# Summing exp through halves added on GpSimd, and reordering the attention stretches

## Chip, cores and metric

The kernel runs on one core of a Trainium2 chip. The metric is the device time of that core in microseconds; lower is better. A run's time is a little longer than the span from the first to the last instruction in its trace.

## What is computed

Two graph layers follow each other on 64 graphs of 256 nodes with 256 features, all in float32. The first layer (adjacency attention, twice, then a feed-forward net with ReLU, with a layernorm after each half) is not touched. The change is in the attention of the second layer, which has eight heads of width 32 and an adjacency matrix that picks, for each pair of nodes, which of several value projections is used:

```python
q = (src @ Wq + bq) ... ; k = (src @ Wk + bk) ...          # split into 8 heads
scores = einsum('bhid,bhjd->bhij', q, k) / sqrt(dh)
attn = softmax(scores, axis=-1)
for r in range(R):
    v_r = (src @ Wv[r] + bv[r]) ...
    mask = (adj_matrix == r)
    out = out + einsum('bhij,bhjd->bhid', attn * mask, v_r)
x = layernorm(src + out @ Wo + bo)
x = layernorm(x + gelu(x @ W1 + b1) @ W2 + b2)
```

The adjacency here holds only 0 and 1, so the kernel uses two value projections: that of relation 0 for every pair of nodes, and the difference of the two on the pairs where the adjacency is 1.

## The kernel before

The 64 graphs are taken in 32 pairs. Each pair goes through one Python generator, `whole_way`: first `gat_layers` (the adjacency attention), then `feed_forward` with ReLU (called ff0 here), then `attention`, then `feed_forward` with Gelu (ff1). Loops over pairs are unrolled; what is generated is one long instruction stream for each engine, and each engine works through its stream in order.

The order of the streams is set by a planner, `in_turn`. It keeps three ways going. A way runs until it yields a triple: the TensorE time that the stretch just emitted is thought to take, a time that has to pass before the way may go on, and optionally a name. Only one way at a time may hold each of the names `gat`, `ff` and `attention`. The planner keeps a clock of its own made of these numbers; at each turn it takes a way that is ready by that clock, and a way in a feed-forward only if no other is ready. So while one pair is in attention, another is in a feed-forward and fills the time that attention's yields leave open: the stretches of `feed_forward` are eight of four matmul passes (`L308`, 1.72) and four of sixteen passes (`L319`, 3.44).

Attention works on four groups, n = 0 to 3, each of one graph b of the pair and one half c of the heads (four heads). The second layer's softmax is computed transposed: a score tile has keys j on the partitions and queries i along the free dimension, in two blocks jc of 128 keys. For one group:

- `scores` (`L360`): eight matmuls with a contraction of 32, four heads side by side, into four PSUM banks; then ScalarE takes exp of each bank into a tile `a` of 128 x 512 (`L365`), the two 256-wide halves being the two blocks of keys.
- `of_relation_1` (`L374`): VectorE multiplies each `a` by the adjacency, giving `m`.
- `sums` (`L381`): eight matmuls with `ones` (128 x 32) on the left sum exp over the keys, two blocks jc accumulated in PSUM, the sum being repeated on the head's 32 partitions.
- `products` (`L388`), with r = 0 on `a` and r = 1 on `m`: sixteen matmuls that add values into the other half of the same bank `po`.
- `divided` (`L394`, `L396`, `L398`): VectorE takes the reciprocal of the sums, keeps a figure that a later range test reads, and multiplies the products by the reciprocal into `oT`.

Around the groups stand the projections of queries and keys (`projected`, `L342`, evicted by ScalarE), the values of each block of keys (`values`, `L335`, evicted by VectorE at `L337` into the tile `v`), and `into_rows` (`L405`), which multiplies `oT` by the output weights, adds the rows (`L266`) and takes a layernorm. The layernorm's reciprocal root is done on GpSimd (`L276`), and so is the addition of a bias to rows when they are transposed (`L292`).

Before the change a stretch of the group loop emits the scores of the next group first, and then the sums and products of this one; the multiplications by the adjacency for the next group are emitted ahead of this group's `divided`:

```python
if not last:
    ahead = scores(*groups[n + 1])
po = bank()
sums(e, po)
products(c, 0, v, e, po)
products(c, 1, v, ms, po)
```

Of the kernel before, what the change touches and what calls it, by code (L numbers as in the profile page):

```python
# [10 lines left out]
F32 = mybir.dt.float32  # L11
# [4 lines left out]
ALU = mybir.AluOpType  # L16
AX = mybir.AxisListType

P = 128
# [10 lines left out]
def two_layers(ctx: ExitStack, tc: tile.TileContext, t: dict, out: bass.AP, flag: bass.AP):  # L30
# [9 lines left out]
    nc = tc.nc  # L40
    B, N, D = out.shape
    NPAIR = B // 2
    KC = D // P
# [4 lines left out]
    DH = D // H  # L48
    HQ = P // DH
# [25 lines left out]
    ones = const.tile([P, DH], F32, name="ones")  # L75
# [28 lines left out]
    with tc.tile_pool(name="setup", bufs=1) as setup, \  # L104
# [11 lines left out]
        for m in range(KC):  # L116
            pw = psetup.tile([P, 512], F32, name="pw")
            for c in range(KC):
                nc.tensor.matmul(pw[:, :D + 4], lhsT=w1T[:, c, m * P:(m + 1) * P], rhs=right[:, c],
                                 start=c == 0, stop=c == KC - 1)  # L120
# [17 lines left out]
    work = ctx.enter_context(tc.tile_pool(name="work", bufs=1))  # L138
# [3 lines left out]
    def bank():  # L142
        return psum.tile([P, 512], F32, name="ps")
# [30 lines left out]
    def done_with(name):  # L174
        del alone[name]

    def of_graph(b):
        return slice(2 * b, 2 * b + 2)
# [84 lines left out]
    def add_rows(y, p, b):  # L263

        rows = y[:, of_graph(b), :].rearrange("p k d -> p (k d)")
        nc.vector.tensor_tensor(rows, p, rows, ALU.add)  # L266

    def layernorm(r, gb, b):
        g, beta = gb
        st, mv = small.tile([P, 2, 6], F32, name="st"), small.tile([P, 2, 2], F32, name="mv")  # L270
        rstd = small.tile([P, 2], F32, name="rstd")
        for j in range(2):
            nc.vector.bn_stats(st[:, j, :], r[:, 2 * b + j, :])  # L273
            nc.vector.bn_aggr(mv[:, j, :], st[:, j, :])
        nc.vector.tensor_scalar(rstd, mv[:, :, 1], EPS, None, ALU.add)  # L275
        nc.gpsimd.tensor_tensor(rstd, rstd, mhalf[:, :2], ALU.pow)  # L276
        for j in range(2):
            row = r[:, 2 * b + j, :]
            nc.vector.scalar_tensor_tensor(row, row, mv[:, j, 0:1], g, op0=ALU.subtract, op1=ALU.mult)
        for j in range(2):  # L280
            row = r[:, 2 * b + j, :]
            nc.vector.scalar_tensor_tensor(row, row, rstd[:, j:j + 1], beta, op0=ALU.mult, op1=ALU.add)
# [11 lines left out]
    def rows_transposed(y, bias):  # L294
        yT = work.tile([P, KC, 512], F32, name="yT", bufs=2)
        for b in range(2):
            transposed(y, yT, bias, b)
            yield 0.5, 0.5 + b * 0.5, None
        return yT
# [31 lines left out]
    def values(v, jc, at, yT):  # L331

        ps = bank()
        for c in range(KC):
            nc.tensor.matmul(ps, lhsT=yT[:, c, at:at + P], rhs=wv[:, c].rearrange("p r m -> p (r m)"),  # L335
                             start=c == 0, stop=c == KC - 1)
        nc.vector.tensor_tensor(v[:, jc], ps, bv, ALU.add)  # L337

    def projected(to, c, yT, w, bias, scale):
        ps = bank()  # L340
        for d in range(KC):
            nc.tensor.matmul(ps, lhsT=w[:, d, c * P:(c + 1) * P], rhs=yT[:, d, :], start=d == 0, stop=d == KC - 1)  # L342
        nc.scalar.activation(to[:, c, :], ps, AF.Identity, bias=bias[:, c:c + 1], scale=scale)

    def attention(y, pair, adjT):


        yT = yield from rows_transposed(y, bo)
        qT, kT, oT = (work.tile([P, KC, 512], F32, name=n) for n in ("qT", "kT", "oT"))

        def values_tile():
            return work.tile([P, 2, 2 * D], F32, name="v", bufs=2)

        def scores(b, c):
            ps = [bank() for _ in range(HQ)]
            for jc in range(2):
                at = b * N + jc * P
                for o in range(HQ):
                    rows = slice(o * DH, (o + 1) * DH)
                    nc.tensor.matmul(ps[o][:, jc * N:(jc + 1) * N], lhsT=kT[rows, c, at:at + P],  # L360
                                     rhs=qT[rows, c, b * N:(b + 1) * N], start=True, stop=True)
            e = []
            for o in range(HQ):
                a = work.tile([P, 512], F32, name="a", bufs=2 * HQ)
                nc.scalar.activation(a, ps[o], AF.Exp)  # L365
                e.append(a)
            return e

        def of_relation_1(b, e):
            adj = adjT[:, of_graph(b), :].rearrange("p k n -> p (k n)")  # L370
            ms = []
            for a in e:
                m = work.tile([P, 512], F32, name="m", bufs=HQ + 2)
                nc.vector.tensor_tensor(m, a, adj, ALU.mult)  # L374
                ms.append(m)
            return ms

        def sums(e, po):
            for jc in range(2):
                for o in range(HQ):  # L380
                    nc.tensor.matmul(po[o * DH:(o + 1) * DH, N:], lhsT=ones, rhs=e[o][:, jc * N:(jc + 1) * N],  # L381
                                     start=jc == 0, stop=jc == 1)

        def products(c, r, v, ms, po):
            for jc in range(2):
                for o in range(HQ):
                    at = r * D + (c * HQ + o) * DH
                    nc.tensor.matmul(po[o * DH:(o + 1) * DH, :N], lhsT=v[:, jc, at:at + DH],  # L388
                                     rhs=ms[o][:, jc * N:(jc + 1) * N],
                                     start=r == 0 and jc == 0, stop=r == 1 and jc == 1)  # L390

        def divided(b, c, po):
            s = work.tile([P, N], F32, name="s", bufs=2)
            nc.vector.reciprocal(s, po[:, N:])  # L394
            junk = work.tile([P, N], F32, name="junk")
            nc.vector.scalar_tensor_tensor(junk, po[:, N:], 1.0, s, op0=ALU.mult, op1=ALU.add,  # L396
                                           accum_out=reach[:, pair, b * KC + c:b * KC + c + 1])
            nc.vector.tensor_tensor(oT[:, c, b * N:(b + 1) * N], po[:, :N], s, ALU.mult)  # L398

        def into_rows(b):  # L400
            ps = bank()
            for j in range(2):
                k = 2 * b + j
                for c in range(KC):
                    nc.tensor.matmul(ps[:, j * D:(j + 1) * D], lhsT=oT[:, c, k * P:(k + 1) * P], rhs=wo[:, c, :],  # L405
                                     start=c == 0, stop=c == KC - 1)
            add_rows(y, ps, b)
            layernorm(y, ln[2], b)

        groups = [(b, c) for b in range(2) for c in range(KC)]  # L410
        v = values_tile()
        projected(qT, 0, yT, wq, bqs, SCALE)
        projected(kT, 0, yT, wk, bk, 1.0)
        yield 3.44, 0.0, None
        values(v, 0, 0, yT)
        yield 1.72, 0.0, None
        e = scores(*groups[0])
        ms = of_relation_1(0, e)
        projected(qT, 1, yT, wq, bqs, SCALE)
        yield 3.0, 0.0, None  # L420
        projected(kT, 1, yT, wk, bk, 1.0)
        values(v, 1, P, yT)
        yield 3.44, 0.0, None
        for n, (b, c) in enumerate(groups):
            last = n == len(groups) - 1
            if not last:
                ahead = scores(*groups[n + 1])
            po = bank()
            sums(e, po)
            products(c, 0, v, e, po)  # L430
            products(c, 1, v, ms, po)
            if not last:
                e, ms = ahead, of_relation_1(groups[n + 1][0], ahead)
            divided(b, c, po)
            yield 3.1 if last else 4.1, 3.2 if last else 0.8, None
            if (b, c) == (0, KC - 1):
                v = values_tile()
                for jc in range(2):
                    values(v, jc, N + jc * P, yT)
                    yield 1.72, 0.0, None  # L440
            if n == 2:
                into_rows(0)
                yield 1.75, 0.0, None
        into_rows(1)
        done_with("attention")
        yield 1.75, 4.5, "ff"

    def whole_way(pair):
        yield 0.0, 0.0, "gat"
        xT, adjT, x = loaded.pop(pair)  # L450
        yield from gat_layers(pair, xT, adjT, x)
        yield from feed_forward(x, ff0, AF.Relu, ln[1])
        yield 3.44, 4.5, "attention"
        yield from attention(x, pair, adjT)
        yield from feed_forward(x, ff1, AF.Gelu, ln[3])
        nc.sync.dma_start(out[2 * pair:2 * pair + 2].rearrange("b (c p) d -> p (b c) d", p=P), x)
        yield 3.44, 0.0, None
# [439 lines left out]
```

## Time and profile before

| | us |
|---|---|
| median of 3 runs (lowest to highest) | 3452.53 (3450.27 to 3455.06) |
| the profiled execution | 3450.98 |
| its span, first to last instruction | 3449.2 |
| TensorE matmul busy in it | 3344.4 (97%) |
| VectorE busy | 1904.6 (55%) |
| ScalarE busy | 1371.0 (40%) |
| GpSimd busy | 481.5 (14%) |

The granted TensorE clock is 0.999 over the span. In lines of the profile, a group of instructions shows the line of the kernel, the engine, the operation, the tile written and the tiles read, the shapes and the count, then the busy time in us and the mean of one instruction in ns, then the idle time of the engine just before them and what ended it. A timeline line begins with the start in us and the length of the merged run of instructions. TensorE's float32 matmuls appear as two passes each, so that eight matmuls are sixteen records. "<-" in brackets names what was waited for.

### The profile page before, as it was taken

How to read it: one execution, taken by the hardware profiler on the slowest of the kernel's cores; microseconds unless marked ns; L12 is line 12 of the kernel's file. 1: busy time of each engine (PE TensorE's matmuls, PEld its weight loads, DVE VectorE, ACT ScalarE, POOL GpSimd, SP SyncE). 2: the span in 40 equal slices, each digit the busy share in tenths (PEclk: the TensorE clock that was granted, in tenths of full speed). 3: DMA queues.
4: the chain of work that ended last, by engine and by line, in shares of the span. 5: the costliest groups of instructions: out<-in, count | busy, mean ns of one | idle time of the engine just before them, and what ended most of it. 6: DMA issues, size and time to landing. Idle time of an engine off the chain costs nothing.

```text
span 3449.2 us, 47284 instructions
## 1 busy us (share of the span) xinstructions
PE 3344.4 (97%) x18698; PEld 2150.5 (62%) x18698; DVE 1904.6 (55%) x4825; ACT 1371.0 (40%) x2586; POOL 481.5 (14%) x646
## 2 busy tenths in 40 slices
PE   7999999999999999999999999999999999999998
PEld 5566665666656566565665666656666566565655
DVE  5655645556456564555645555465554655546455
ACT  4343343433434334343444434444253442534332
POOL 0201111011110111111111111111111111111110
PEclk9999999999999999999999999999999999999999
DMA  5000010000100001000000100001000010000000
GB/s 166 7 25 19 13 37 7 25 19 13 37 7 25 25 7 37 7 28 23 20 25 7 41 10 25 19 7 43 7 25 19 7 43 7 25 19 1 13 1 14
DMA packets 66868, 78.22 MB, mean 23 GB/s; under 512 B 3280, under 2 KB 57680, under 8 KB 66640
## 3 DMA queue, kind: packets, MB, share of 16 engines
q1 hardware_dynamic: 66640, 75.13, 7.0%
q8 instruction: 150, 2.46, 0.3%
q14 instruction: 78, 0.64, 0.1%
HBM read 58.34 MB, written 16.78 MB: 22 GB/s over the span
## 4 chain that ended last, share of the span: by engine, by line
PE 87%; ACT 9%; DVE 2%; DMA 1%; issue 0%; SPq 0%; POOL 0%; POOLq 0%; DVEq 0%
PE ps L319 26%; PE ps L308 23%; PE ps L342 7%; PE ps L335 6%; PE ps L388 6%; PE ps L360 4%; PE ps L381 4%; PE ps L253 3%; PE ps L405 3%; ACT L189 2%; ACT yT L290 2%; PE ps L241 2%; PE ps L227 2%; PE ps L289 1%; ACT ff L311 1%; DVE e L206 1%
## 5 line engine op out<-in xcount | busy, mean ns | idle before, releaser
L276 POOL TENSOR_TENSOR rstd<-rstd,mhalf 128x2 f32<-128x2 f32 x256 | 206.1, 805 | 2729.3 <-DVE rstd L275 2713.4
L308 PE MATMUL ps<-yT,w_L_gnn_W 128*128 128x512 f32 x1024 | 482.7, 602 | 14.2 <-ACT yT L290 12.5
L308 PE MATMUL ps<-yT,w_L_gnn_w_ff 128*128 128x512 f32 x1024 | 482.5, 602 | 14.1 <-ACT yT L290 12.5
L319 PE MATMUL ps<-w_L_gnn_w_ff,ff 128*128 128x256 f32 x2048 | 450.2, 379 | 0.0
L319 PE MATMUL ps<-w_L_gnn_W,ff 128*128 128x256 f32 x2048 | 449.9, 379 | 0.0
L319 PEld LDWEIGHTS ps<-w_L_gnn_W,ff 128*128 128x128 f32 x2048 | 389.1, 190 | 66.6 <-issue 15.3
L319 PEld LDWEIGHTS ps<-w_L_gnn_w_ff,ff 128*128 128x128 f32 x2048 | 389.0, 190 | 66.0 <-issue 14.8
L374 DVE TENSOR_TENSOR m<-a,adjT 128x512 f32<-128x512 f32 x512 | 327.0, 688 | 175.6 <-ACT a L365 134.9
L266 DVE TENSOR_TENSOR x<-ps,x 128x512 f32<-128x512 f32 x256 | 176.1, 688 | 444.3 <-PE ps L319 330.7
L311 ACT ACTIVATE ff<-ps,c_L_gnn_b_ff 128x512 f32<-128x512 f32 x256 | 176.0, 687 | 448.2 <-PE ps L308 448.2
L365 ACT ACTIVATE a<-ps 128x512 f32<-128x512 f32 x512 | 264.4, 602 | 216.3 <-PE ps L360 216.1
L337 DVE TENSOR_TENSOR v<-ps,b_L_gnn_bv 128x512 f32<-128x512 f32 x128 | 88.1, 689 | 400.5 <-PE ps L335 400.5
L308 PEld LDWEIGHTS ps<-yT,w_L_gnn_W 128*128 128x128 f32 x1024 | 183.0, 190 | 199.2 <-issue 174.1
L308 PEld LDWEIGHTS ps<-yT,w_L_gnn_w_ff 128*128 128x128 f32 x1024 | 183.1, 190 | 198.9 <-issue 174.2
L290 ACT ACTIVATE yT<-ps 128x512 f32<-128x512 f32 x192 | 110.2, 592 | 479.8 <-PE ps L289 479.8
L311 ACT ACTIVATE ff<-ps,c_L_gnn_b 128x512 f32<-128x512 f32 x256 | 175.9, 687 | 292.8 <-PE ps L308 292.4
L335 PE MATMUL ps<-wv,yT 128*128 128x512 f32 x512 | 235.4, 592 | 0.0
L229 ACT ACTIVATE xw<-ps 128x260 f32<-128x260 f32 x128 | 45.7, 379 | 456.0 <-PE ps L227 456.0
L394 DVE RECIPROCAL s<-ps 128x256 f32<-128x256 f32 x128 | 224.0, 1750 | 0.0
L273 DVE BATCH_NORM_STATS2 st<-x 128x6 f32<-128x256 f32 x512 | 192.7, 418 | 8.6
L206 DVE SCALAR_TENSOR_TENSOR e<-ps,ratio,up 128x256 f32<-128x256 f32 x256 | 115.7, 475 | 141.2 <-ACT up L201 141.2
L335 PEld LDWEIGHTS ps<-wv,yT 128*128 128x128 f32 x512 | 97.3, 190 | 122.5 <-issue 122.2
(81 smaller groups left out, 4290.1 us busy)
## 6 DMA issues: line engine op xcount, KB each, us to landing
xT<-in_xT SPq DMA_DIRECT2D x32, 512.0 KB, 4.6
adjT<-in_adjT SPq DMA_DIRECT2D x32, 512.0 KB, 3.9
x<-in_x SPq DMA_DIRECT2D x32, 512.0 KB, 4.2
out<-x SPq DMA_DIRECT2D x32, 512.0 KB, 3.2
w_L_gnn_w_ff<-in_L_gnn_w_ff SPq DMA_DIRECT2D x2, 1024.0 KB, 11.3
w_L_gnn_W<-in_L_gnn_W SPq DMA_DIRECT2D x2, 1024.0 KB, 7.0
wv<-in_L_gnn_Wv SPq DMA_DIRECT2D x2, 256.0 KB, 7.1
w_L_gnn_W1T<-in_L_gnn_W1T SPq DMA_DIRECT2D x1, 256.0 KB, 6.1
```

What stands on the lines that cost most here:

```text
L273: nc.vector.bn_stats(st[:, j, :], r[:, 2 * b + j, :])
L276: nc.gpsimd.tensor_tensor(rstd, rstd, mhalf[:, :2], ALU.pow)
L290: nc.scalar.activation(yT[:, :, b * N:(b + 1) * N], pt.rearrange("p (c n) -> p c n", c=KC), AF.Copy)
L308: nc.tensor.matmul(p1, lhsT=w1[:, c, m * P:(m + 1) * P], rhs=yT[:, c, :], start=c == 0, stop=c == KC - 1)
L311: nc.scalar.activation(h, p1, func, bias=b1[:, m:m + 1])
L319: nc.tensor.matmul(p2[:, j * D:(j + 1) * D], lhsT=f[m][:, k * P:(k + 1) * P], rhs=w2[:, m, :], start=m == 0, stop=m == NF - 1)
L335: nc.tensor.matmul(ps, lhsT=yT[:, c, at:at + P], rhs=wv[:, c].rearrange("p r m -> p (r m)"), start=c == 0, stop=c == KC - 1)
L342: nc.tensor.matmul(ps, lhsT=w[:, d, c * P:(c + 1) * P], rhs=yT[:, d, :], start=d == 0, stop=d == KC - 1)
L365: nc.scalar.activation(a, ps[o], AF.Exp)
L374: nc.vector.tensor_tensor(m, a, adj, ALU.mult)
L388: nc.tensor.matmul(po[o * DH:(o + 1) * DH, :N], lhsT=v[:, jc, at:at + DH], rhs=ms[o][:, jc * N:(jc + 1) * N], start=r == 0 and jc == 0, st ...
L394: nc.vector.reciprocal(s, po[:, N:])
```

## The change

The two 256-wide halves of each exp tile are first added on GpSimd into a new tile `halves` (128 x 256, six buffers), four additions for each group. The sum over keys is then one matmul with `ones` for each head instead of two accumulated ones. In the group loop a stretch now emits the group's own sums, products and `divided` first, and then the scores of the next group, their exp, the additions on GpSimd and the multiplications on VectorE. The yields, which the planner reads, are set anew.

```diff
+        def halves_added(e):
+            hs = []
+            for a in e:
+                h = work.tile([P, N], F32, name="halves", bufs=HQ + 2)
+                nc.gpsimd.tensor_tensor(h, a[:, :N], a[:, N:], ALU.add)
+                hs.append(h)
+            return hs
...
-        def sums(e, po):
-            for jc in range(2):
-                for o in range(HQ):
-                    nc.tensor.matmul(po[o * DH:(o + 1) * DH, N:], lhsT=ones, rhs=e[o][:, jc * N:(jc + 1) * N],
-                                     start=jc == 0, stop=jc == 1)
+        def sums(hs, po):
+            for o in range(HQ):
+                nc.tensor.matmul(po[o * DH:(o + 1) * DH, N:], lhsT=ones, rhs=hs[o], start=True, stop=True)
...
         e = scores(*groups[0])
-        ms = of_relation_1(0, e)
+        hs, ms = halves_added(e), of_relation_1(0, e)
...
         for n, (b, c) in enumerate(groups):
+            po = bank()
+            sums(hs, po)
+            products(c, 0, v, e, po)
+            products(c, 1, v, ms, po)
+            divided(b, c, po)
             last = n == len(groups) - 1
             if not last:
-                ahead = scores(*groups[n + 1])
-            po = bank()
-            sums(e, po)
-            products(c, 0, v, e, po)
-            products(c, 1, v, ms, po)
-            if not last:
-                e, ms = ahead, of_relation_1(groups[n + 1][0], ahead)
-            divided(b, c, po)
-            yield 3.1 if last else 4.1, 3.2 if last else 0.8, None
-            if (b, c) == (0, KC - 1):
+                e = scores(*groups[n + 1])
+                hs, ms = halves_added(e), of_relation_1(groups[n + 1][0], e)
+            if last:
+                yield 2.8, 4.8, None
+            elif n == 1:
+                yield 3.7, 0.0, None
                 v = values_tile()
                 for jc in range(2):
                     values(v, jc, N + jc * P, yT)
-                    yield 1.72, 0.0, None
-            if n == 2:
+                    yield 1.72, jc * 0.2, None
+            elif n == 2:
+                yield 3.7, 0.0, None
                 into_rows(0)
-                yield 1.75, 0.0, None
+                yield 1.75, 1.9, None
+            else:
+                yield 3.7, 3.6, None
```

## The prediction

> **What bounds the kernel now.** I read the page's busy times and its chain first, then the waits of TensorE, then the timeline of one attention. From the page:
>
> ```profile
> PE 3344.4 (97%) x18698; PEld 2150.5 (62%) x18698; DVE 1904.6 (55%) x4825; ACT 1371.0 (40%) x2586; POOL 481.5 (14%) x646
> ...
> PE 87%; ACT 9%; DVE 2%; DMA 1%; issue 0%; SPq 0%; POOL 0%; POOLq 0%; DVEq 0%
> ```
>
> TensorE carries 87% of the chain. Its waits sum to only some 92 us, nearly all in the other layer:
>
> ```profile
> PE ps L199 <- ACT rise L189: 29.6, 46, 0.9
> PE ps L308 <- ACT yT L290: 25.0, 34, 0.7
> PE ps L253 <- ACT xw L212: 21.0, 16, 3.0
> ```
>
> No line of attention's group loop (L360, L381, L388) is there. TensorE runs through attention without a gap, as this timeline of one group shows (scores, sums, two products):
>
> ```profile
> 1047.41 1.15 PE L360 MATMUL ps<-qT,kT 32*128 32x256 f32 x16
> 1048.48 1.07 PE L381 MATMUL ps<-a,ones 128*32 128x256 f32 x16
> 1049.37 1.05 PE L388 MATMUL ps<-a,v 128*32 128x256 f32 x16
> 1050.23 1.05 PE L388 MATMUL ps<-m,v 128*32 128x256 f32 x16
> ```
>
> From start to start the scores take 1.07 us, the sums 0.89, the products 0.86. So a matmul removed is time gained, if nothing new is waited for.
>
> **What the Trainium skill says.** "TensorE: Matmul & The Clock Gate", Part 3 (Packing small matmuls): matmuls on different column strips run side by side. The trace agrees: sixteen passes of 379 ns in 0.89 us, four at a time. "GPSIMD Engine Reference", Engine selection: a two-input elementwise operation is about twice as slow there as on VectorE. Here 0.73 against 0.48 us for 128x256, the one fused on VectorE. "SBUF — State Buffer", Who interferes with whom: a VectorE instruction with two SBUF inputs and a GpSimd instruction that reads SBUF exclude each other. The trace agrees, and the forecast hangs on it. First VectorE, then GpSimd:
>
> ```profile
> 97.03 0.91 DVE L279 SCALAR_TENSOR_TENSOR x<-x,mv,b_L_gnn_g_ln 128x256 f32<-128x256 f32 x1
> 97.86 0.69 DVE L275 TENSOR_SCALAR rstd<-mv 128x2 f32<-128x2 f32 x1
> 98.47 1.03 DVE L279 SCALAR_TENSOR_TENSOR x<-x,mv,b_L_gnn_g_ln 128x256 f32<-128x256 f32 x1
> ```
>
> ```profile
> 96.25 2.96 POOL L292 TENSOR_TENSOR x<-x,b_L_gnn_bo 128x256 f32<-128x256 f32 x4
> ```
>
> L279 has a median of 0.47 us but takes 0.91 and 1.03 beside these additions, so it stood still for about 0.45 and 0.55; L275 takes 0.69 for 0.16. One addition was held up too (0.91 for 0.72). Taking each stall off, the engines alternate: an addition holds the other off for about 0.57 us, a 256-wide L279 for 0.33. A 512-wide multiplication at L374 has two SBUF inputs and 256 more elements; its line (0.69 against 0.42 us for 256 wide at L398) adds 0.27, so I put its turn at 0.60 us.
>
> **The change, part by part.** Four groups by 32 pairs are 128 groups.
>
> (1) Sums. Half of sixteen passes goes: four rounds of 0.215 us become two, 0.89 becomes 0.46. 128 x 0.43 = **-55 us**, all on the path. The weight loads (109 ns each) halve with them and lie beside.
>
> (2) Switches between array shapes. Before, scores then sums cost 1.07 - 0.86 = 0.21 more than plain streaming, and products then L308 about 0.11 (0.97 start to start). After, products are followed by scores, which the trace doesn't show. Bounds 0.11 to 0.25; I take +0.04 for each of 96: **+4 us** (0 to 13).
>
> (3) What now covers the exp. I stepped `in_turn` through the yields of both versions (for the order alone); for the version before it gives the trace's order. After the change there stands between every group's scores and its sums: for n = 0, L342 twice and L335; n = 1, three L308; n = 2, L335 twice and one L308; n = 3, L405 and one L319 stretch. Each is 5.16 to 5.2 us, with a switch 5.3. Counting from the first score pass as t = 0, the sums can start at 1.07 + 5.3 = 6.4, the products of r = 0 at 6.87, of r = 1 at 7.7.
>
> The supply: in the trace the first exp starts 1.16 after the scores, lasts 0.6, and the next follow each 0.49 (1033.70 for scores at 1032.54). So `a` is ready at 1.8, 2.3, 2.8, 3.25. GpSimd is free (L276 and L292 come elsewhere in the order).
>
> VectorE's queue holds `divided` of the group just multiplied ahead of the four multiplications: from 0.2, L394 1.78, L396 0.35, L398 0.34, to 2.67. By turns then: additions 1.85 to 2.4 and 2.5 to 3.1, multiplication to 3.7, addition to 4.3, multiplication to 4.9, addition to 5.45, the last two multiplications to 6.65. The halves are ready at 5.6, before 6.4; `m` at 6.7, before 7.7. **Groups n = 1 and n = 3: nothing**, hidden under the feed-forward's L308 or L319, with 0.8 us to spare.
>
> (4) Group n = 2. Behind those multiplications stand the two evictions of the new values (L337, 0.69, spaced 0.62): ready at 7.35 and 8.0. Products want the first at 6.87 and the second at 7.3. TensorE waits 0.53, then, as the first block of products runs to 7.83, 0.2 more: 0.73 x 32 = **+23 us** (nothing without exclusion, 1.35 each or 43 if turns cost 0.73 and 0.69 in full).
>
> (5) Group n = 0. No `divided` stands ahead, so both engines start at 1.8 and alternate. If VectorE is first, the last half is ready at 6.65, 0.25 late; if GpSimd is first, all are in time, and the eviction of `v` at 6.5 too. 0.15 x 32 = **+5 us** (0 to 16).
>
> (6) Another interleaving. By the same stepping, the adjacency layers of 19 pairs instead of 15 lie beside a Gelu feed-forward, 13 instead of 17 beside a ReLU one. In the timeline TensorE stands still 0.52 + 0.92 + 1.20 = 2.64 us in the first kind (at 1080, 1093, 1098) and 0.53 in the second (at 1125), since exp and Gelu need table loads in turn. 4 x 2.1 = **+8.5 us** (0 to 10). The table loads themselves fall from 218 to 182 by the stepping, 46 us of ScalarE that was not in the way.
>
> (7) Costed at nothing: the 512 additions (512 x 0.73 = 374 us of GpSimd, beside TensorE); `into_rows(1)`, which needs the last `divided`: behind the multiplications (6.65), L266 and its layernorm (4.0 in the trace) and 2.55, at 13.2, while TensorE comes there at 6.4 + 2.2 + 6.9 = 15.5; the waits of L374 for a free `m` (40.6 us on VectorE), which go, since products now come first; the halves' six buffers, freed before the next scores. No DMA is moved, and SP's queue is not passed.
>
> Sum: -55 + 4 + 23 + 5 + 8.5 = -14.5. Against the profiled execution's 3450.98 (its span and 1.8 around it) that is 3436.5; the median of the runs is 1.5 higher, so I forecast **3438**.
>
> **Rivals.**
>
> *Full cover.* Exclusion may bite less on L374 than on L279. In the trace before, L374 never exceeds 0.695 us, but no addition ran beside it, so that says little. Then (4) and (5) vanish: 3452.5 - 55 + 4 + 8.5 = **3410**.
>
> *Slower: the turns on the SBUF port cost more.* Place: the four additions and four multiplications behind each exp. If a turn holds for the whole length (0.73 + 0.69 = 1.42 instead of 1.17), n = 2 waits 1.35 and n = 0 about 1.0: 32 x 2.35 = 75 us, net -55 + 75 + 12.5: **3485**. If an addition on the exp tile takes 1.0 us, halves come at 1.85 + 4.0 + 1.2 = 7.05 in the other groups too, 0.64 late. 64 x 0.64 = 41 us more gives about 3525. It decides once waits pass 55 - 12.5 = 42 us, 1.3 us for each pair, against the 0.9 that I count; in the groups n = 1 and 3 from 0.84 us for an addition on. For it: each step above hangs on a chain of eight turns with under 1 us to spare. Against it: both held-up kinds of instruction fit 0.57 and 0.33.
>
> *The change gives nothing:* (4) to (6) just reach the gain, about **3452**. That the sums don't halve is hardly possible: with four strips full, TensorE takes 0.215 us a round in sums and products alike.
>
> **How the numbers follow.** Turns as I price them, 0.45 (3420 to 3455, the likeliest's own range, of which 0.27 lies under the bound); full cover, 0.2; dearer turns, 0.35. About 0.2%, 7 us, is what a measurement of this kernel can tell from no change. Faster: 0.27 + 0.2 = 0.47. Same: 0.16 of the first and 0.03 of the last, 0.19. Slower: 0.02 + 0.32 = 0.34. The range, 3400 to 3495, runs from full cover with no cost of (2) and (6) to dearer turns in the groups n = 0 and 2, and leaves out those in all groups.
>
> **What would show it.** Right: sums of eight records, 0.46 us; L374 and the additions longer than 0.69 and 0.73 beside each other; new waits of TensorE at L388 for the eviction L337 once in each pair, near 0.7 us; 182 table loads. Wrong: sums waiting for GpSimd in groups 1 to 3 (the dearer turns), no wait at L388 at all (full cover), or products to scores over 0.25.

## The result, and the profile after

The changed kernel takes 3469.72 us (median of six runs, 3468.94 to 3471.69) where the kernel before took 3453.42 beside it (3450.27 to 3455.06). The ratio is 1.0049, 95% interval 1.0036 to 1.0062: **slower by half a per cent**. The forecast was 3438 and a gain. The profiled execution took 3470.03, with a span of 3468.2; the span before was 3449.2, so 19.0 us are to be explained. Of these, 3.4 arise in the first 54 us, in which TensorE still runs the same passes in both kernels, at a mean granted clock of 0.94 in this execution against 0.97 in the one before.

In the page of the changed kernel, first the busy times, then the shares of the chain that ended last:

```profile
PE 3330.9 (96%) x17674; PEld 2134.8 (62%) x17674; DVE 2106.4 (61%) x4825; ACT 1321.3 (38%) x2550; POOL 1034.4 (30%) x1158
...
PE 75%; ACT 10%; DVE 8%; POOL 4%; issue 2%; DMA 0%; ACTq 0%; SPq 0%; POOLq 0%; DVEq 0%
```

The 1024 passes went, as planned (18698 to 17674), and so did 36 table loads of ScalarE (218 to 182, as forecast). But TensorE's share of the chain fell from 87% to 75%: VectorE and GpSimd, 2% and 0% before, are now on the path. The waits of TensorE in the changed kernel say where (total us, times, longest):

```profile
PE ps L199 <- ACT rise L189: 29.5, 40, 1.1
PE ps L308 <- ACT yT L290: 28.1, 44, 0.7
PE ps L253 <- ACT xw L212: 25.4, 20, 2.6
PE ps L388 <- POOL halves L373: 16.9, 33, 0.5
...
PE ps L394 <- DVE v L337: 8.4, 21, 0.4
```

Two lines of the group loop are there, where before there was none: the sums (`L388`) wait for GpSimd's halves, 33 times, and the products (`L394`) for the eviction of the values, 21 times. The numbers 33 and 21 are the clue. There are 32 pairs; 33 is three groups of 11 attentions, and 21 the rest. A wait shows only partly under this heading, since the load of the weights (PEld) waits ahead of its pass. So I measured whole blocks in TensorE's timeline: from the first sums pass of a group to the first pass after its products, for all 128 groups.

| block, us | n = 0 | n = 1 | n = 2 | n = 3 | sum of 128 |
|---|---|---|---|---|---|
| before | 2.73 | 2.73 | 2.73 | 2.73 | 349.1 |
| after, 21 attentions beside a ReLU feed-forward | 2.43 | 2.30 | 2.98 | 2.30 | |
| after, 11 attentions beside a Gelu feed-forward | 3.70 | 2.30 | 3.70 | 3.68 | 357.3 (all) |

A block that waits for nothing takes 2.30 (128 of them sum to 293.9 in a run shown below). The wait in the first kind of attention is 0.13 + 0.68 = 0.81 us, in the second 1.40 + 1.40 + 1.38 = 4.18. Together 21 x 0.81 + 11 x 4.18 = 63 us. The forecast had 0.88 for each of 32, or 28.

The timeline of the changed kernel in an attention beside ReLU, group n = 2, rows of TensorE, GpSimd and VectorE (start, duration, operation, idle before):

```profile
1050.69 1.15 PE L360 MATMUL ps<-qT,kT 32*128 32x256 f32 x16
...
1052.57 3.67 POOL L373 TENSOR_TENSOR halves<-a 128x256 f32<-128x256 f32 x4 [4.49 <-ACT a L365]
...
1053.30 4.10 DVE L382 TENSOR_TENSOR m<-a,adjT 128x512 f32<-128x512 f32 x4
...
1057.11 0.64 PE L388 MATMUL ps<-halves,ones 128*32 128x256 f32 x8
...
1058.14 1.15 PE L394 MATMUL ps<-a,v 128*32 128x256 f32 x16 [0.40 <-DVE v L337]
1059.11 1.05 PE L394 MATMUL ps<-m,v 128*32 128x256 f32 x16
1060.08 1.15 PE L360 MATMUL ps<-qT,kT 32*128 32x256 f32 x16
```

This is what the prediction's step (4) describes: sums 6.42 after the scores, no wait at them, then products that wait for `L337`. The same group beside Gelu:

```profile
1114.73 1.15 PE L360 MATMUL ps<-qT,kT 32*128 32x256 f32 x16
...
1115.93 1.28 ACT L365 ACT_TABLE_LOAD   x1 [2.70 <-PE ps L360]
...
1117.22 2.06 ACT L365 ACTIVATE a<-ps 128x512 f32<-128x512 f32 x4
...
1117.85 4.09 DVE L382 TENSOR_TENSOR m<-a,adjT 128x512 f32<-128x512 f32 x4 [0.42 <-ACT a L365]
1117.90 4.63 POOL L373 TENSOR_TENSOR halves<-a 128x256 f32<-128x256 f32 x4 [5.76 <-ACT a L365]
...
1121.16 0.91 PE L388 MATMUL ps<-halves,ones 128*32 128x256 f32 x6
...
1122.58 0.40 PE L388 MATMUL ps<-halves,ones 128*32 128x256 f32 x1 [0.52 <-POOL halves L373]
...
1124.86 1.15 PE L360 MATMUL ps<-qT,kT 32*128 32x256 f32 x16
```

ScalarE stood idle for 2.70 us, and only when the scores were there did it begin to load the table of exp. The first exp starts 2.49 us after the scores, not 1.21 as beside ReLU: 1.28 us later. The additions lose more than that. In the group beside ReLU the first two run alone, while VectorE is still in `divided`, and take 0.73 us each (four in 3.67); here `divided` is nearly over when the first exp tile is ready, all four alternate with multiplications, and they take 4.63. So the last half is ready 7.80 us after the scores instead of 5.57, which is 2.23 later. The sums could start at 6.42; their last pass ends at 1123.2 instead of near 1121.8.

Before, ScalarE began each load as soon as it was free: 33 of the 49 started 0.9 us or more ahead of the scores, the other 16 (one in each attention beside Gelu, for group n = 2) 0.8 us or more after them, behind an eviction of Gelu. Groups by form, row of the table loads at exp's line; first the kernel before, then the changed one (count, busy, mean ns, idle time before them and what ended it):

```profile
L365 ACT ACT_TABLE_LOAD x49 | 62.9, 1283 | 0.9
```

```profile
L365 ACT ACT_TABLE_LOAD x33 | 42.3, 1283 | 98.0 <-PE ps L360 98.0
```

There are fewer loads, as forecast, but ScalarE is idle for 98.0 us ahead of them, until TensorE's scores arrive; before it was 0.9. The traces also hold the instructions that only wait, and there the reason can be read. Tile `a` had two kinds of readers, TensorE and VectorE; GpSimd is a third, so an exp that reuses the tile has one more engine to wait for. One wait stays on the exp itself, and the others are issued as separate waits ahead of it. Before, what stood ahead was VectorE's, long over, and at all 49 loads the wait for the scores stayed on the exp; the table load stands between the two. Now, at all 33 loads, the waits for VectorE and for TensorE, which includes the scores, both stand ahead of the load, and GpSimd's is on the exp.

### The profile page after: what moved, and what is told of

Its sections match the earlier page's. It is cut to its first block, busy times and chain, and to the rows that moved or that the text cites. A ratio compares the mean times of both kernels' runs of the same rounds, so it can differ in the third digit from the quotient of the medians.

```text
span 3468.2 us, 45608 instructions
## 1 busy us (share of the span) xinstructions
PE 3330.9 (96%) x17674; PEld 2134.8 (62%) x17674; DVE 2106.4 (61%) x4825; ACT 1321.3 (38%) x2550; POOL 1034.4 (30%) x1158
## 4 chain that ended last, share of the span: by engine, by line
PE 75%; ACT 10%; DVE 8%; POOL 4%; issue 2%; DMA 0%; ACTq 0%; SPq 0%; POOLq 0%; DVEq 0%
PE ps L319 24%; PE ps L308 20%; PE ps L394 7%; PE ps L342 5%; POOL halves L373 4%; PE ps L360 3%; PE ps L253 3%; DVE m L382 3%; PE ps L335 3%; PE ps L411 3%; PE ps L227 2%; ACT L189 2%; ACT yT L290 2%; PE ps L388 2%; PE ps L241 1%
## 5 line engine op out<-in xcount | busy, mean ns | idle before, releaser
L373 POOL TENSOR_TENSOR halves<-a 128x256 f32<-128x256 f32 x512 | 536.6, 1078 | 719.1 <-ACT a L365 719.1
L276 POOL TENSOR_TENSOR rstd<-rstd,mhalf 128x2 f32<-128x2 f32 x256 | 214.1, 837 | 1576.5 <-DVE rstd L275 1565.1
L382 DVE TENSOR_TENSOR m<-a,adjT 128x512 f32<-128x512 f32 x512 | 523.8, 1082 | 56.5 <-ACT a L365 56.4
L308 PE MATMUL ps<-yT,w_L_gnn_w_ff 128*128 128x512 f32 x1024 | 474.7, 599 | 16.6 <-ACT yT L290 15.4
L308 PE MATMUL ps<-yT,w_L_gnn_W 128*128 128x512 f32 x1024 | 471.9, 597 | 13.7 <-ACT yT L290 12.7
L319 PE MATMUL ps<-w_L_gnn_w_ff,ff 128*128 128x256 f32 x2048 | 456.5, 380 | 0.0
L319 PE MATMUL ps<-w_L_gnn_W,ff 128*128 128x256 f32 x2048 | 452.0, 380 | 0.0
L319 PEld LDWEIGHTS ps<-w_L_gnn_W,ff 128*128 128x128 f32 x2048 | 388.2, 190 | 65.8 <-issue 14.6
L319 PEld LDWEIGHTS ps<-w_L_gnn_w_ff,ff 128*128 128x128 f32 x2048 | 387.3, 190 | 64.7 <-issue 13.5
L308 PEld LDWEIGHTS ps<-yT,w_L_gnn_w_ff 128*128 128x128 f32 x1024 | 186.7, 191 | 208.0 <-issue 181.6
L308 PEld LDWEIGHTS ps<-yT,w_L_gnn_W 128*128 128x128 f32 x1024 | 187.8, 190 | 197.4 <-issue 169.4
L337 DVE TENSOR_TENSOR v<-ps,b_L_gnn_bv 128x512 f32<-128x512 f32 x128 | 84.9, 682 | 290.7 <-PE ps L335 290.7
```

The source lines that it names most:

```text
L308: nc.tensor.matmul(p1, lhsT=w1[:, c, m * P:(m + 1) * P], rhs=yT[:, c, :], start=c == 0, stop=c == KC - 1)
L319: nc.tensor.matmul(p2[:, j * D:(j + 1) * D], lhsT=f[m][:, k * P:(k + 1) * P], rhs=w2[:, m, :], start=m == 0, stop=m == NF - 1)
L373: nc.gpsimd.tensor_tensor(h, a[:, :N], a[:, N:], ALU.add)
```

## The experiments

All ratios are to the kernel before, run beside on the same chip; its median there was about 3454. Blocks are measured as above.

**1. The load alone taken out of the way.** A tiny exp, of one column, is put ahead of each group's scores. It carries the table load, and waits for nothing late. All else is the changed kernel.

```python
+ early, latest = const.tile([P, 1], F32, name="early"), [None]
  ...
+ latest[0] = h                    # in feed_forward
  ...
+ nc.scalar.activation(early, latest[0][:, :1], AF.Exp, scale=0.0)   # first in scores()
```

> The changed kernel with one tiny exp (128x1) issued on ScalarE behind the last feed-forward eviction ahead of each group's scores, so that the table load of exp comes there and not behind the wait for the scores. Theory A (in attentions beside a Gelu feed-forward the load of 1.28 us stands behind the wait for the scores, exp is late, and the sums of three of four groups wait 1.27 + 0.72 + 1.37 = 3.36 us more than beside ReLU; 11 such attentions, 37 us): 3470 - 37 = 3433, and the blocks of sums and products beside Gelu take the 2.43, 2.30, 2.98 and 2.30 us that they take beside ReLU. Rival B (ScalarE's own backlog of Gelu evictions, or GpSimd's turns, make the halves late there): 3465 to 3472, blocks of 3.7 us as they are.

It took 3437.12 us (3431.41 to 3438.53), ratio 0.9951 [0.9934, 0.9967]. ScalarE's and TensorE's rows of its timeline, same group beside Gelu:

```profile
1103.68 1.28 ACT L357 ACT_TABLE_LOAD   x1
1104.97 0.20 ACT L357 ACTIVATE early<-ff 128x1 f32<-128x1 f32 x1
...
1106.37 2.06 ACT L368 ACTIVATE a<-ps 128x512 f32<-128x512 f32 x4 [1.20 <-issue]
```

```profile
1105.16 1.15 PE L363 MATMUL ps<-qT,kT 32*128 32x256 f32 x16
...
1111.58 0.64 PE L391 MATMUL ps<-halves,ones 128*32 128x256 f32 x8
...
1112.62 1.14 PE L397 MATMUL ps<-a,v 128*32 128x256 f32 x16 [0.40 <-DVE v L339]
```

The load is over before the scores start at 1105.16, exp starts 1.21 after them, and the group beside Gelu now behaves like one beside ReLU. Blocks are 2.4, 2.3, 3.0 and 2.3 in all 32 attentions and sum to 319.9; after, it was 357.3. **The late load was worth 37 us in blocks and 33 in time** (some 5 us come back at other lines, mostly in the adjacency layers), and the forecast of 3438 is met once it is gone.

**2. The new order alone.** Sums as before, eight matmuls over `a` (sixteen passes), no halves; yields and order as changed.

```python
- sums(hs, po)
+ sums(e, po)                      # two blocks jc, as before
- hs, ms = halves_added(e), of_relation_1(...)
+ ms = of_relation_1(...)
```

> The changed order of the stretches and its yields, but the sums are taken over exp itself with eight matmuls, and nothing is added on GpSimd. Theory A (the waits come from the halves and the multiplications sharing the port, and from the late load, which only the third wait of exp brings about): no waits in the groups, load not late; what is left is the price of the other interleaving, which in the changed kernel's trace is about 11 us (19 lost = -55 sums + 63 waits + 11): 3464. Rival C (the order itself makes exp or the multiplications late): waits of TensorE at the products remain, 3475 or more. Rival D (the order is free): 3453.

3459.84 us, ratio 1.0017 [1.001, 1.0024], between theory A and rival D. Blocks are 2.7 everywhere: no wait. Two engines read `a` again, and the table load is early again, though order and yields are those of the changed kernel:

```profile
L365 ACT ACT_TABLE_LOAD x33 | 42.3, 1283 | 0.6
```

So it is not the order that delays the load. The order by itself costs 5.9 us by the medians, outside the blocks. The spans of the profiled executions differ by more, 9.6 us (3458.8 against 3449.2), but 4.2 of these arise in the first 54 us, where both run the same passes. From start to start, the passes of `L319` take 890.3 us instead of 884.1: 31 runs of them now end at column-strip sums and 31 begin behind column-strip products, where before none did. The waits at `L253` in the adjacency layers are 4 us longer (25.3 against 21.0), but all other lines together take no more time than before.

**3. The halves added on VectorE.** One word of the changed kernel: `nc.gpsimd` becomes `nc.vector` in `halves_added`.

> The changed kernel with the halves added on VectorE instead of GpSimd. Theory A (adding on GpSimd saves VectorE nothing, since each addition holds it off for as long as it would take itself; and exp still has three waits here, so its load stays late): beside ReLU only group n = 2 waits, 0.6 us; beside Gelu the multiplications end at 7.4 after the scores, n = 0 waits 0.8, n = 2 1.45, n = 3 0.1: 21 x 0.6 + 11 x 2.35 = 38 us of waits against 63: 3446, between 3438 and 3455. Rival B (GpSimd is simply too slow for these additions): no waits, 3407. Rival E (GpSimd does take work off VectorE): VectorE becomes late, 3480 or more.

3432.22 us (3432.0 to 3432.46), ratio 0.9942 [0.9925, 0.9958], lower than the range given; rivals B (3407) and E (3480) are both out. VectorE's rows of its timeline in a group n = 2 beside Gelu:

```profile
1106.78 0.42 DVE L373 TENSOR_TENSOR halves<-a 128x256 f32<-128x256 f32 x1 [0.42 <-ACT a L365]
1107.13 0.68 DVE L382 TENSOR_TENSOR m<-a,adjT 128x512 f32<-128x512 f32 x1
1107.73 1.09 DVE L373 TENSOR_TENSOR halves<-a 128x256 f32<-128x256 f32 x3
1108.73 1.89 DVE L382 TENSOR_TENSOR m<-a,adjT 128x512 f32<-128x512 f32 x3
1110.54 1.28 DVE L337 TENSOR_TENSOR v<-ps,b_L_gnn_bv 128x512 f32<-128x512 f32 x2
```

VectorE does all four additions and four multiplications from 1106.78 to 1110.54, in 3.76 us. By turns with GpSimd the changed kernel needs, in the Gelu group shown above, 4.63 for its additions, and VectorE 4.09 for the multiplications alone. **The offload saved nothing**: an addition on GpSimd holds VectorE up longer than VectorE would take for it. The load is late here too,

```profile
L365 ACT ACT_TABLE_LOAD x33 | 42.3, 1283 | 92.4 <-PE ps L360 92.4
```

so it is not GpSimd as such, nor a third engine: only TensorE and VectorE read `a` here, but at all 33 loads the waits for both stand ahead, and a third wait, for ScalarE's own counter, is on the exp. What puts that third wait there is open. Blocks are 2.3/2.6, 2.3, 2.7/3.2 and 2.3 (ReLU/Gelu where they differ) and sum to 316.2: the faster supply makes up for part of the delay. I had expected 38 us of waits and it was 22.

**4. The late load and the queue behind n = 2 both cured.** Kernel 1, and for n = 1 only the halves are emitted at once, two of the four multiplications following each eviction of the values.

```python
- hs, ms = halves_added(e), of_relation_1(groups[n + 1][0], e)
+ hs = halves_added(e)
+ if n != 1: ms = of_relation_1(groups[n + 1][0], e)
  ...
- values(v, jc, N + jc * P, yT)
+ with tc.issue_after(values(v, jc, N + jc * P, yT).ins):   # values returns its eviction
+     ms += of_relation_1(1, e[2 * jc:2 * jc + 2])
```

> The kernel of the early load, and in group n = 1's stretch the eviction of each half of the new values stands ahead of two of the four multiplications, not behind all four. Theory A (the products of group n = 2 wait 0.68 us only because the evictions of the values queue behind the multiplications): 3433 - 32 x 0.68 = 3411, no wait of TensorE at the products, block n = 2 at 2.3 us. Rival F (the turns on the port are what is late, so that the multiplications, now later, hold up the products of r = 1 instead): 3425 to 3435.

3411.21 us, ratio 0.9883 [0.9867, 0.99]. Blocks are 2.4, 2.3, 2.3 and 2.3 and sum to 297.9: the wait of group n = 2 was the queue on VectorE, as step (4) had it.

**5. The same with the halves on VectorE** (kernel 4, `nc.vector` in `halves_added`).

> The changed kernel with all three: early load of exp, evictions of the values between the multiplications, and the halves on VectorE. Theory A: against the same on GpSimd (3411) only group n = 0's wait of 0.13 us goes, 32 x 0.13 = 4 us: 3407; what stays against the old order on VectorE is the price of the changed interleaving, 6 to 8 us. Rival (VectorE, now at its fullest, is late somewhere): 3415 or more.

3407.76 us, ratio 0.9868 [0.9851, 0.9884]. All blocks are 2.30, in sum 293.9; so the halved sums are worth 349.12 - 293.86 = 55.3 us.

**6 and 7. The halves in the old order.** The kernel before (scores of the next group, then sums and products of this one, old yields) with halved sums; 6 with the additions on GpSimd, 7 on VectorE.

```python
- sums(e, po)
+ sums(hs, po)
- e, ms = ahead, of_relation_1(groups[n + 1][0], ahead)
+ e, hs, ms = ahead, halves_added(ahead), of_relation_1(groups[n + 1][0], ahead)
```

> The order and the yields of the kernel before, with only the halves added on GpSimd and the sums over them: the other half of the change alone. Theory A (turns on the port and a late load of exp): the last half is ready 6.5 us after the first score pass beside ReLU and 7.8 beside Gelu, where exp waits for its table; the sums of group n = 1 come at 6.35, of n = 3 at 7.1, of n = 0 at 7.5, of n = 2 at 9.8. Waits: beside ReLU 0.25 for each attention, beside Gelu 1.45 + 0.7 + 0.3 = 2.45, 16 attentions each: 43 us, so 3454 - 55 + 43 = 3442, between 3434 and 3456; two load kinds of block in n = 1 and n = 3. Rival (with scores a group ahead everything is hidden, so the loss lay in the order): 3399, no waits for halves.

> The order and the yields of the kernel before, with the halves added on VectorE and the sums over them. Theory A (VectorE alone works off four additions and four multiplications in 3.76 us, less than the 4.6 by turns): ready 5.6 us after the first score pass beside ReLU and, with exp late by its table, the halves at about 4.9 and the multiplications at 6.85 beside Gelu; needed at 6.35 and 7.7 at the earliest: no waits, 3454 - 55 = 3399. Rival (VectorE gets late for the evictions of the values and the divisions, which queue behind): waits of TensorE at the products or at L411, 3410 or more.

Both expectations were **missed**; on VectorE it is the rival named, waits at `L411`, that came. On GpSimd: 3457.55, ratio 1.0012 [1.0005, 1.0019]; on VectorE: 3448.66 (3443.89 to 3457.8), ratio 0.999 [0.9981, 0.9999]. The blocks do gain, to 316.1 and 294.7, but TensorE waits elsewhere. Waits of TensorE in kernel 7:

```profile
PE ps L411 <- DVE oT L404: 35.4, 30, 2.9
PE ps L199 <- ACT rise L189: 29.5, 46, 0.9
```

`L411` is `into_rows`, which needs the last group's `divided`. From start to start its 512 passes take 159.9 us instead of 113.6 (149.8 in kernel 6). Before, this was met by a hair. The last `divided` and the output matmuls behind it in the kernel before, VectorE and TensorE:

```profile
1062.32 0.42 DVE L398 TENSOR_TENSOR oT<-ps,s 128x256 f32<-128x256 f32 x1
```

```profile
1062.85 1.89 PE L405 MATMUL ps<-w_L_gnn_Wo,oT 128*128 128x256 f32 x8
```

It ended at 1062.74, and the matmuls start at 1062.85. In kernel 7 the same group:

```profile
1066.45 0.42 DVE L404 TENSOR_TENSOR oT<-ps,s 128x256 f32<-128x256 f32 x1
```

```profile
1064.38 0.59 PE L411 MATMUL ps<-w_L_gnn_Wo,oT 128*128 128x256 f32 x2
1066.93 1.56 PE L411 MATMUL ps<-w_L_gnn_Wo,oT 128*128 128x256 f32 x6 [1.96 <-DVE oT L404]
```

VectorE had four more additions and a late exp (beside Gelu it starts 2.49 us after the scores for three of the four groups here too), and so came later to what stands ahead of the last reciprocal in both kernels: the first half's layernorm and a reduction of the next adjacency. Of the 46 us that `L411` lost, 36 fall in the 16 attentions beside Gelu and 10 in those beside ReLU, where exp is not late (22 and 14 in kernel 6). That points to the late load in the old order as well, but no run cures it alone there. Another 9 us of kernel 7's profiled execution are no waits: `L319` took 893.6 us, at a mean granted clock of 0.994 against 0.998 in kernel 6.

**8 and 9. The old order with a longer gap.** Kernels 7 and 6, with one number changed, the time that the last group's yield leaves to others before `into_rows(1)`:

```python
- yield 3.1 if last else 4.1, 3.2 if last else 0.8, None
+ yield 3.1 if last else 4.1, 6.0 if last else 0.8, None
```

> The order of the kernel before with the halves on VectorE, and one number changed: the time that the planner lets pass after the last group's stretch is 6.0 instead of 3.2, so that two stretches of L319, not one, stand between the last products and the multiplication by the output weights. Theory A (what took the gain in the old order is that VectorE, with four additions more in each group, brings the last division too late for that multiplication: 46 us of waits there, 113.6 to 159.9 us): the waits go, 3449 - 46 = 3403, and with the changed interleaving up to 6 us more. Rival (VectorE as a whole is too late and the wait moves on to the next transposition): 3430 or more.

> The order of the kernel before with the halves on GpSimd, and the same number changed. Theory A: of the 3457.6 the 36 us that the multiplication by the output weights waited go, and the 22 us of waits at the sums and products stay: 3422. Rival (the waits at sums and products grow in their stead): 3440 or more.

On VectorE 3399.01 us (3395.16 to 3399.62), ratio **0.9844 [0.9828, 0.986], the best of all**, below both the kernel before and the changed one. On GpSimd 3418.6, ratio 0.9897 [0.9881, 0.9914]. The waits of TensorE on VectorE's version:

```profile
PE ps L199 <- ACT rise L189: 29.5, 46, 0.9
PE ps L308 <- ACT yT L290: 25.0, 34, 0.7
PE ps L253 <- ACT xw L212: 20.6, 16, 2.7
```

`L411` is gone and the rest is what the kernel before had. Of kernel 9's gain over kernel 6 (39 us), the waits at `L411` account for 149.8 - 113.5 = 36 us; the 22 us of waits in its blocks stay, about its distance to kernel 8 (19.6). So the 55 us of the halved sums can be had whole, without the new order (3454.22 - 3399.01 = 55.2). The new order does not bring a longer cover for the additions: in it the sums come 6.42 us after the scores, in kernel 8 between 6.36 and 9.8. What it brings is its 4.8 for the last yield, which hides the late `divided` (`L411` takes 114.1 us in the changed kernel).

## Why the prediction was wrong, step by step

The sum against the measured terms of the span:

| step | forecast | measured |
|---|---|---|
| (1) halved sums | -55 | -55.3 (349.2 - 293.9) |
| (2) switches | +4 | 0 where the step placed it; +6 at `L319` |
| (4), (5) waits at n = 2, n = 0 | +28 | +26 (32 x 0.81) |
| (3), (6) late table load | 0 | **+37** (11 x (4.18 - 0.81)) |
| (6) adjacency layers | +8.5 | +1 (with all other lines) |
| first 54 us, the same passes | 0 | +3.4 |
| sum | -14.5 | +18 (the span: +19.0) |

**The step that failed is (3), with the remark on table loads in (6).** Step (3) took the supply of exp from one trace, "in the trace the first exp starts 1.16 after the scores", and used it for every group; step (6) called the loads "46 us of ScalarE that was not in the way". Both held only while the load was done ahead of the scores. A third wait on exp put the load behind them in 33 groups. Exp came 1.28 us later, and in groups n = 2 and 3 the additions also lost the time that step (3) let GpSimd work alone, so that the last half came 2.23 later, against a cover with 0.85 us to spare: that leaves 1.38, the wait measured at n = 3. I had counted how many loads would go and not where the rest would stand. The trace of before showed that this matters. For the scores that start at 1038.26 (group n = 2 beside Gelu) ScalarE's rows are:

```profile
1038.37 0.69 ACT L311 ACTIVATE ff<-ps,c_L_gnn_b 128x512 f32<-128x512 f32 x1 [1.30 <-PE ps L308]
1039.07 1.28 ACT L365 ACT_TABLE_LOAD   x1
1040.37 2.07 ACT L365 ACTIVATE a<-ps 128x512 f32<-128x512 f32 x4
```

Here the first exp comes 2.11 us after the scores, not 1.16. It cost nothing then, as these sums come 10.2 us after the scores. "ScalarE: Activation LUTs", What ACT_TABLE_LOAD costs, gives 1283 ns for the load, as measured here, and adds a drain of 1380 ns for each switch; in this trace the exp starts 0.01 us after the load's end (1115.93 + 1.28, then 1117.22), and in the rows above the load 0.01 us after the eviction's end, so no run here shows that drain: a switch cost 1.3 us.

**Right beside ReLU.** Steps (4) and (5) said 0.73 and 0.15; it was 0.68 and 0.13. The exclusion on the SBUF port, from "SBUF — State Buffer", Who interferes with whom, is confirmed, with multiplications and additions at medians of 1.21 and 1.17 us where alone they take 0.69 and 0.73. The page has the other engine blocked for the whole instruction in VectorE's two-port modes, and says of two SBUF inputs only that they contend; turns of 0.57 and 0.60, under the full lengths, gave these waits to within 0.05 us. Kernel 4 took away the queue of step (4) alone, and its wait went.

**Step (1)** was exact. **Step (2)**: products to scores take 0.97 from start to start, as products to `L308` did, so nothing was added there; but the reordering put more switches beside `L319`, 6 us, which no step had. **Step (6)** had the sign of the adjacency waits right and twice the size (at `L253` 25.4 us against 21.0), but in time it was nearly nothing: from start to start all lines outside the blocks and `L319` take about 1 us more, behind the first 54 us. In kernel 1 they take 7 more.

**The rivals.** "Dearer turns" forecast the slower side, for another reason: it put late sums down to longer turns. Sums did wait for GpSimd, the mark named for it, but kernel 1 shows that the turns were as priced, and that the whole chain began later. Full cover, 3410, was reached in the new order only by kernels 4 and 5, which made that cover.

Still open is how much of the loss of kernels 6 and 7 an early load alone would have cured. The loads are late in kernels 6 to 9 too, but in kernel 8 only one of the 128 blocks waits (by 0.8 us), and `L411` not at all. It wasn't tried with an early load.

## What to carry to other kernels

Before giving a tile one more reader, see what writes the tile and count the writer's waits afterwards: it can get one more, with a new engine (GpSimd here) or without (kernel 3), and where the writer is an activation, a table load can be pushed behind its inputs; here a one-column activation ahead of them took 0.2 us and kept the load early. Look for this in every group of a trace, not in one. Additions beside two-input VectorE work were better kept on VectorE here, as an addition on GpSimd cost VectorE more than doing it; try that first where VectorE has time. And when a block on the critical engine gets shorter, list every consumer that was met by a hair, and lengthen the gap ahead of it before reordering anything.

## What was not expected of the hardware

- The table load itself takes 1.283 us in every kernel; what changed is where it may begin. With two waits for an exp in the new order ScalarE is idle for 0.6 us ahead of 33 loads, with three for 98.0 (the third for GpSimd) or 92.4 (for ScalarE's own counter).
- An addition of 128x256 takes 0.73 us on GpSimd alone and 1.17 (median) beside two-input multiplications; on VectorE it takes 0.42, and 0.34 from start to start when it is one of a row. In each of the four pairs of kernels that differ in this alone (the changed kernel and 3, 4 and 5, 6 and 7, 9 and 8) VectorE's version was faster, by 37.5, 3.5, 8.9 and 19.6 us.
- Around matmuls on column strips a switch costs about 0.1 us: 0.11 from products to `L308`, and the same from products to scores, on row strips.
